# A gated recurrence and a feed-forward layer: a first state from 40 steps instead of 48, and the input products in five visits

## The chip, the core and the metric

The kernel runs on one core of a Trainium2 chip. The core has five engines with a queue each: TensorE (PE in the profile; its weight loads are shown apart as PEld), VectorE (DVE), ScalarE (ACT), GpSimd (POOL) and SyncE (SP). Each takes its instructions in the order in which they were written, and waits on semaphores where an instruction needs what another engine or a transfer makes. SBUF holds the tiles in use. PE writes its products to PSUM, from which DVE and ACT move them out. The metric is the time of one execution on the device, in microseconds (us), as the median of repeated runs. The profile is that of one more execution.

## The reference

Two sequences of 4096 vectors x of 256 numbers go through a gated recurrence with 64 states, a residual, a layer norm, a feed-forward layer with binarized weights, a residual and a layer norm.

```python
u = x @ W_in + b_in
g = sigmoid(x @ W_gate + b_gate)
def step(h_prev, inputs):
    u_t, g_t, x_t = inputs
    h_t = tanh(h_prev @ A + u_t @ Bm)
    y_t = h_t @ C.T + u_t @ D.T
    y_t = g_t * y_t + (1.0 - g_t) * x_t
    return h_t, y_t
...
x = layernorm(x + (ys @ W_out + b_out + x))
h = gelu(x @ bw1.T + b1)          # bw = mean|w| of its row * sign(w)
x = layernorm(x + (h @ bw2.T + b2))
```

## The kernel before, in words

**Segments and chunks.** Each sequence is cut into 64 segments of 64 steps. All 128 segments (two sequences times 64) are stepped side by side, so that one step of the recurrence is one product of 128 x 128 (`steps`, line 157: the matrix `ab` holds A above Bm, the moving operand `st[:, j]` holds h above u) and one tanh on ACT (line 158). Four steps of all segments are a chunk: `SPC` = 4, `NC` = 16 chunks, each of 512 vectors. A segment does not know its first state. It is therefore first run over its last `WARM` = 48 steps from zero. The state that this leaves at the end of segment k is copied (`first_states`, line 161) as the first state of segment k + 1, and then all 64 steps are run. At the end `compare` (lines 163 to 173) counts the entries where the last state of a segment agrees with the first state that was used for the next one within 2^-20. If not all agree, a serial branch at the end of the kernel does the recurrence and all chunks anew. There are 48 + 64 = 112 steps. The warm steps begin at chunk `FIRST` = (64 - 48) / 4 = 4.

**u.** The steps of a chunk need its u, which `u_of_chunks` (line 124) makes from x in transposed form (`x_tiles`): products on PE with 64 output columns (line 131), half of them into the upper and half into the lower 64 partitions of a PSUM tile of tag "h", then one eviction for each chunk that adds the bias and writes into `st` (lines 142 to 144, DVE except for one on ACT). One call takes one or two chunks.

**The opening.** The order of all instructions is written out by hand. `emit` (its costs are in `COST`) adds up the cost of the PE work that goes by and puts one step of the recurrence behind it whenever the sum passes a pace. In the opening this gives one step behind each part of the gate products. `parts` takes such parts from `gates` (its product is line 313; three 128-wide blocks to a part, two halves of 512 columns by two contractions to a chunk). The chunks come in the order 4, 5, 6, 7, 0, 1, 2, 3, 8, 9, 10 and on. A u visit is followed by one step. Between them stand the transfers on SP's queue: `load_xT` (x of a chunk, 512 KB, eight buffers), `load_weights`, `load_w` with `prepare_w` (signs and mean magnitudes of w1 and w2 on DVE), `halve_weights`, and for the first chunks `load_u`, `load_h` (u and h of a chunk into the tile hu), `load_n` (x by rows, xn).

**The chunks.** A chunk then goes through `mix` (line 374, ps_y = h C + u D, and d on DVE), `mix_end` (the gate, lines 386 and 389), `project` (line 399, W_out), the layer norm (`stats1`, `shift`, `norm`), a transpose (`turn` by PE for the first and the last chunks, `blocks` by DVE and sixteen transfers for the others, line 455), `up` (line 486), `low`, `down` (line 528), `add`, `stats` and `store`. POOL adds the bias rows (line 359) and takes the powers of the layer norms (line 265). The main loop runs over the chunks; steps of the recurrence that are left stand in it by up to four a chunk, and stop when all 112 are done. x of a chunk is loaded there a second time (`load_x`, line 338), and a third time for gates that are made there (`load_gate_x`).

**PSUM.** p_s holds the step's product. p_m holds one tile of two banks (tag "m": ps_y, ps_t). p_1 holds three tiles of one bank (tag "h": ps_u, ps_g, ps_h). p_2 holds one tile of two banks (tag "o": ps_o, and ps_z at first).

Of the kernel before, what the change touches and what calls it, by code (L numbers as in the profile page):

```python
# [8 lines left out]
FP = mybir.dt.float32  # L9
FR = mybir.dt.float32r  # L10
I32 = mybir.dt.int32
AF = mybir.ActivationFunctionType
ALU = mybir.AluOpType
# [3 lines left out]
P = 128  # L17
B, T, DM, S, H = 2, 4096, 256, 64, 1024
KD = DM // P
KH = H // P  # L20
SEG = 64
L = T // SEG
WARM = 48
N = 512
W = B * SEG
SPC = N // W
NC = L // SPC
TB = N // P
# [4 lines left out]
EARLY = 500  # L33
TOP, LOW = slice(0, S), slice(S, P)
# [3 lines left out]
def gated_recurrence_then_binary_ffn(  # L38
# [61 lines left out]
    def load_xT(c, pieces=1):  # L100
        x_tiles[c] = xp.tile([P, KD, N], FP, tag="xt", name=f"xt{c}", bufs=XTB)
        for k in range(pieces):
            cut = slice(k * KD // pieces, (k + 1) * KD // pieces)
            nc.sync.dma_start(out=x_tiles[c][:, cut, :], in_=xT[c][:, cut, :])
# [16 lines left out]
    nc.vector.tensor_scalar(bg_c, bias_c[:, 1 : 1 + KD], 0.5, None, ALU.mult)  # L121


    def u_of_chunks(*chunks):

        n = N * len(chunks) // 2
        parts = [(chunks[0], 0), (chunks[1], 0) if len(chunks) == 2 else (chunks[0], 1)]
        ps = p_1.tile([P, N], FP, tag="h", name=f"ps_u{chunks[0]}")
        for k in range(KD):
            for (c, i), r in zip(parts, (LOW, TOP)):  # L130
                nc.tensor.matmul(  # L131
                    ps[r, :n],
                    w_in[k],
                    x_tiles[c][:, k, bass.ts(i, n)],
                    start=k == 0,
                    stop=k == KD - 1,
                    skip_group_check=True,
                )
        for (c, i), r in zip(parts, (LOW, TOP)):
            to = u_of[:, bass.ds(c * SPC + i * n // W, n // W)].rearrange("p j b k -> p (j b k)")  # L140
            if r is TOP and c == FIRST:
                nc.scalar.activation(to, ps[r, :n], AF.Identity, bias=bin_c[r, :])
            else:
                nc.vector.tensor_scalar(to, ps[r, :n], bin_c[r, :], None, ALU.add)
        have_u.update(chunks)
        yield


# [31 lines left out]
    def load_weights():  # L180
        nc.sync.dma_start(out=cd, in_=CD)
        nc.sync.dma_start(out=w_out, in_=W_out)
        nc.sync.dma_start(out=bo_r, in_=b_out.partition_broadcast(P))
        nc.sync.dma_start(out=b2_r, in_=b2.partition_broadcast(P))

    def halve_weights():
        nc.vector.tensor_scalar(w_out, w_out, 0.5, None, ALU.mult)
        nc.vector.tensor_scalar(bo_r, bo_r, 0.5, None, ALU.mult)
# [12 lines left out]
    def load_w(n):  # L201
        half = bass.ts(n % 2, KH // 2)
        if n < 2:
            t = wk.tile([P, H], FP, tag="h", name=f"w1t{n}")
            nc.sync.dma_start(out=t, in_=w1T[:, n, :])
            t2 = wk.tile([P, KH // 2, DM], FP, tag="xhi", name=f"w1n{n}")
            nc.sync.dma_start(out=t2, in_=w1[:, half, :])
            w_tiles[n] = t, t2
        else:
            t = wk.tile([P, KH // 2, DM], FP, tag="h", name=f"w2t{n}")  # L210
            nc.sync.dma_start(out=t, in_=w2T[:, half, :])
            w_tiles[n] = t, None

    def prepare_w(n):
        half = bass.ts(n % 2, KH // 2)
        t, t2 = w_tiles[n]
        if n < 2:
            nc.vector.tensor_reduce(al1[:, half], t2, AX.X, ALU.add, apply_absolute_value=True)
            nc.vector.tensor_scalar(al1[:, half], al1[:, half], 1.0 / DM, None, ALU.mult)
            signs(sg1[:, n, :], t, f"a{n}")  # L220
        else:
            nc.vector.tensor_reduce(
                al2[:, n % 2, :],
                t.rearrange("p j d -> p d j"),
                AX.X,
                ALU.add,
                apply_absolute_value=True,
            )
            if n == 3:
                nc.vector.tensor_add(al2[:, 0, :], al2[:, 0, :], al2[:, 1, :])  # L230
            signs(
                sg2[:, half, :].rearrange("p j d -> p (j d)"),
                t.rearrange("p j d -> p (j d)"),
                f"b{n}",
            )
# [64 lines left out]
    def gates(chunks, size, x_of=lambda c: x_tiles[c.c]):  # L300

        room = size[0]
        for c in chunks:
            xt_ = x_of(c)
            c.t = wk.tile([P, KD, N], FP, tag="tg", name=f"tg{c.nm}", bufs=TGB)
            for m in range(KD):
                ps = p_1.tile([P, N], FP, tag="h", name=f"ps_g{c.nm}_{m}")
                for k in range(KD):
                    i = 0
                    while i < TB:  # L310
                        n = min(room, TB - i)
                        cut = bass.ds(i * P, n * P)
                        nc.tensor.matmul(  # L313
                            ps[:, cut],
                            w_gate[:, k, bass.ts(m, P)],
                            xt_[:, k, cut],
                            start=k == 0 and i == 0,
                            stop=k == KD - 1,
                            skip_group_check=True,
                        )  # L320
                        i += n
                        room -= n
                        if k == KD - 1 and i == TB:
                            later(c.tanh, m, ps)
                        if room == 0:
                            yield
                            room = size[0]
# [336 lines left out]
    def emit(what, pieces, pace=5600):  # L664
        nonlocal since
        for _ in pieces:
            since += COST.get(what, 0)
            if since >= pace:
                since = min(since - pace, pace // 2)
                if ready():  # L670
                    next_steps()
# [5 lines left out]
    def do(i, what, *args, pace=5600):  # L677
        if not 0 <= i < len(ch):
            return
        if what == "load":  # L680
            need = WARM + (ch[i].c + 1) * SPC
            while done < need:
                next_steps()
            ch[i].load_u()
            ch[i].load_h()
        elif what in ("load_n", "load_x", "load_gate_x"):
            getattr(ch[i], what)()
        else:
            emit(what, getattr(ch[i], what)(*args), pace)

    size = [3]
    stream = gates([ch[i] for i in (4, 5, 6, 7, 0, 1, 2, 3, 8, 9, *range(10, NC))], size)

    def parts(n, pace):
        emit("part", (next(stream) for _ in range(n)), pace)

    ET = mybir.EngineType
    with tc.manual_schedule(engines={ET.PE, ET.Activation, ET.DVE, ET.Pool, ET.SP}):
# [1 line left out]
        for c in range(FIRST + 1, FIRST + 6):  # L700
            load_xT(c)
        idle_products(7)
        emit("u", u_of_chunks(FIRST), 1 << 30)
        since = 0
        pairs = [(5, 6), (7, 8), (9, 10), (11, 12), (13, 14), (), (1, 2)]
        loads = [[10, 11], [12, 13], [14, 15, 0], [1, 2], [3], [], []]
        for n, pair in enumerate(pairs):
            before = 2 if n == 0 else 1
            parts(before, EARLY)
            if pair:  # L710
                emit("", u_of_chunks(*pair))
                if pair == (13, 14):
                    emit("", u_of_chunks(15, 0))
                emit("u", [None], EARLY)
            for c in loads[n]:
                load_xT(c)
            if n == 0:
                load_weights()
            if n == 3:
                halve_weights()  # L720
            if n >= 5:
                load_xT(n + 3)
                ch[n - 4].load_n()
                if n == 5:
                    ch[0].load_u()
                else:
                    ch[0].load_n()
                    ch[1].load_u()
                    ch[2].load_u()
            for i in range(7 - before):  # L730
                if 1 <= n < 5 and i == 0:
                    load_w(n - 1)
                if 2 <= n < 6 and i == 3:
                    prepare_w(n - 2)
                parts(1 if (n, i) != (6, 5) else 0, EARLY)
        assert done >= WARM + SPC, done
        emit("u", u_of_chunks(3), EARLY)
        for i in range(4):
            ch[i].xt = x_tiles[i]
        ch[0].in_x = ch[1].in_x = True  # L740
        do(10, "load_gate_x")
        parts(1, 600)
        do(0, "mix", pace=850)
        do(0, "mix_end")
# [25 lines left out]
        do(0, "rest")  # L770
        next(mixed)
        parts(3, 1700)
        for i in (4, 5):
            do(i, "load_x")
        end = len(ch) - 1
        parts_met = compare()
        since = -1 << 40
# [161 lines left out]
```

## Time and profile before

| what | value |
|---|---|
| median of 3 runs | 436.59 us (435.91 to 437.37) |
| the profiled execution | 438.51 us |
| its span, first to last instruction | 436.6 us |
| mean granted clock of TensorE | 0.993 |
| u products (L131), 6 to 75 us | 66 instructions, 15.1 us busy |
| gate products (L313), 6 to 75 us | 154 instructions, 43.1 us busy |
| step products (L157), 6 to 75 us | 124 instructions, 25.1 us busy |
| step tanh (L158), whole span | 112, median 270 ns, last start at 329.1 us |
| transfers of x in 512 KB (L104, L338) | 35, median 4.5 us from issue to landing |

How to read it: an fp32 product appears as two instructions on PE, so 62 steps are 124. Busy times of PE overlap, because a product is followed by the next before its end; the chain of waits shows what each adds. "Idle before, releaser" gives the time an engine stood before an instruction, and what ended it. The forty slices of the page show where the transfers are: nearly all of the first 55 us.

```profile
DMA  8877814400152624262426242524233232311102
```

### The profile page before, as it was taken

Reading aid. Unit: us, or ns where it says so; the run is one execution under the profiler, and the core shown is the slowest. Engines: PE = TensorE matmul, PEld = TensorE weight load, DVE = VectorE, ACT = ScalarE, POOL = GpSimd, SP = SyncE. Lnnn points to the kernel's source line nnn. Section 1 sums busy time; section 2 is a strip of 40 time slices with the busy share of each in tenths; the row PEclk is TensorE's granted clock in tenths of the full one; section 3 lists DMA queues with packets and bytes.
Section 4 is the critical chain, followed back from the end, with each engine's and each line's share of the span. In section 5 each row is a group of like instructions: output and inputs, shape, how many; then the busy total and the mean of one; then the engine's idle time right before and its main releaser. Section 6 shows DMA issues by size and latency. Waiting matters only on the chain.

```text
span 436.6 us, 6829 instructions
## 1 busy us (share of the span) xinstructions
PE 426.7 (98%) x2406; PEld 346.5 (79%) x2406; DVE 332.9 (76%) x569; ACT 285.3 (65%) x480; POOL 159.7 (37%) x176
## 2 busy tenths in 40 slices
PE   8999999999999999999999999999999999999992
PEld 6666666788887979787979797988888888888982
DVE  0235846886889898888888797979797979789684
ACT  2344352485768676767677776777768585849881
POOL 1000050373064545353524443444443444315513
PEclk9999999999999999999999999999999999999997
DMA  8877814400152624262426242524233232311102
GB/s 291 271 266 286 293 24 147 156 2 0 36 158 63 197 68 150 68 183 80 138 74 191 79 141 71 182 82 115 99 106 110 61 110 60 110 37 50 48 2 101
DMA packets 31479, 51.34 MB, mean 118 GB/s; under 512 B 5328, under 2 KB 19664, under 8 KB 31440
## 3 DMA queue, kind: packets, MB, share of 16 engines
q1 hardware_dynamic: 30864, 50.48, 36.5%
q8 instruction: 21, 0.34, 0.3%
q10 hardware_dynamic: 576, 0.37, 0.3%
q14 instruction: 18, 0.15, 0.1%
HBM read 31.43 MB, written 8.39 MB: 91 GB/s over the span
## 4 chain that ended last, share of the span: by engine, by line
PE 87%; DVE 4%; SPq 2%; ACT 2%; DMA 2%; issue 1%; POOL 1%; POOLq 0%; DVEq 0%
PE ps_h L486 24%; PE ps_o L528 23%; PE ps_g L313 13%; PE ps_z L399 12%; PE ps_s L157 6%; PE ps_y L374 6%; PE ps_u L131 3%; SPq L455 2%; DMA w_gate<-in_W_gate 1%; ACT xn L278 1%; DVE hlo L512 1%; DVE xlo L467 1%; DVE bs_a L255 1%; PE ps_t L430 1%; DMA hu<-st 1%
## 5 line engine op out<-in xcount | busy, mean ns | idle before, releaser
L528 PE MATMUL ps_o<-sg,hhi 128*128 128x256 f32 x496 | 120.7, 284 | 0.1
L528 PE MATMUL ps_o<-sg,hlo 128*128 128x256 f32 x496 | 117.9, 279 | 0.1
L496 ACT ACTIVATE h<-ps_h,bias_c,al 128x512 f32<-128x512 f32 x128 | 95.2, 770 | 15.0 <-PE ps_h L486 11.5
L528 PEld LDWEIGHTS ps_o<-sg,hhi 128*128 128x128 f32 x496 | 93.5, 188 | 1.6 <-DVE o L544 0.5
L528 PEld LDWEIGHTS ps_o<-sg,hlo 128*128 128x128 f32 x496 | 93.4, 188 | 1.5 <-DVE hlo L512 0.3
L486 PE MATMUL ps_h<-xhi,sg 128*128 128x512 f32 x256 | 92.6, 443 | 0.0
L359 POOL TENSOR_TENSOR xn<-xn,bo_r 128x256 f32<-128x256 f32 x64 | 58.1, 941 | 89.7 <-DMA xn<-in_x 84.1
L512 DVE TENSOR_TENSOR hlo<-h,hhi 128x1024 fp32r<-128x1024 f32 (+1 forms) x65 | 78.6, 1227 | 4.8 <-ACT hhi L505 4.6
L486 PE MATMUL ps_h<-xlo,sg 128*128 128x512 f32 x256 | 79.8, 393 | 0.0
L505 ACT CAST hhi<-h 128x1024 fp32r<-128x1024 f32 (+1 forms) x65 | 67.4, 1039 | 2.0
L313 PE MATMUL ps_g<-xt,w_gate 128*128 128x384 f32 (+3 forms) x212 | 67.5, 432 | 0.3 <-DMA w_gate<-in_W_gate 0.3
L265 POOL TENSOR_TENSOR rs_b<-rs_b,neg_half 128x4 f32<-128x4 f32 (+1 forms) x17 | 28.1, 1655 | 107.0 <-DVE rs_b L264 102.0
L486 PEld LDWEIGHTS ps_h<-xhi,sg 128*128 128x128 f32 x256 | 46.6, 189 | 18.6 <-issue 11.2
L158 ACT ACTIVATE st<-ps_s 64x128 f32<-64x128 f32 x112 | 30.0, 267 | 47.0 <-PE ps_s L157 46.6
L486 PEld LDWEIGHTS ps_h<-xlo,sg 128*128 128x128 f32 x256 | 48.1, 188 | 10.8
L157 PEld LDWEIGHTS ps_s<-st,wab 128*128 128x128 f32 x224 | 38.2, 191 | 21.5 <-ACT st L158 10.4
L359 POOL TENSOR_TENSOR xn<-xn,b_r 128x256 f32<-128x256 f32 x64 | 53.3, 863 | 1.9 <-PE ps_t L430 1.9
L399 PE MATMUL ps_z<-w_out,tg 128*128 128x256 f32 x224 | 50.7, 379 | 0.0
L399 PEld LDWEIGHTS ps_z<-w_out,tg 128*128 128x128 f32 x224 | 41.4, 190 | 5.1
L157 PE MATMUL ps_s<-st,wab 128*128 128x128 f32 x224 | 44.5, 280 | 0.0
L265 POOL TENSOR_TENSOR rs_a<-rs_a,neg_half 128x4 f32<-128x4 f32 x16 | 17.1, 1070 | 68.3 <-DVE rs_a L264 68.3
L278 ACT ACTIVATE xn<-xn,nm_a,rs_a 128x256 f32<-128x256 f32 x60 | 31.2, 590 | 16.1 <-DVE nm_a L270 16.1
(79 smaller groups left out, 484.3 us busy)
## 6 DMA issues: line engine op xcount, KB each, us to landing
xt<-in_xT SPq DMA_DIRECT2D x35, 512.0 KB, 4.5
xn<-in_x SPq DMA_DIRECT2D x16, 512.0 KB, 3.3
out_y<-xn SPq DMA_DIRECT2D x15, 512.0 KB, 2.6
xlo<-xb SPq DMA_DIRECT2D x208, 32.0 KB, 1.9
hu<-st SPq DMA_DIRECT2D x32, 128.0 KB, 2.3
w1t<-in_w1T SPq DMA_DIRECT2D x2, 512.0 KB, 5.4
w1n<-in_w SPq DMA_DIRECT2D x2, 512.0 KB, 7.1
w2t<-in_w2T SPq DMA_DIRECT2D x2, 512.0 KB, 5.7
```

What stands on the lines that cost most here:

```text
L157: nc.tensor.matmul(p_h, ab, st[:, j].rearrange("p b k -> p (b k)"), start=True, stop=True)
L158: nc.scalar.activation(h_of[:, j + 1].rearrange("p b k -> p (b k)"), p_h[TOP, :], AF.Tanh)
L265: nc.gpsimd.tensor_tensor(rs, rs, neg_half[:, cut], ALU.pow)
L278: nc.scalar.activation(r, r, AF.Identity, bias=self.sh[:, i : i + 1], scale=rs)
L313: nc.tensor.matmul(ps[:, cut], w_gate[:, k, bass.ts(m, P)], xt_[:, k, cut], start=k == 0 and i == 0, stop=k == KD - 1, skip_group_check=True,)
L359: nc.gpsimd.tensor_tensor(r[:, i, :], r[:, i, :], row, ALU.add)
L399: nc.tensor.matmul(self.ps_z[:, i, :], self.y[:, k, bass.ts(i, P)], w_out[:, k, :], start=k == 0, stop=k == KD - 1,)
L486: nc.tensor.matmul(ps, sg1[:, k, bass.ts(j, P)], part[:, k, :], start=n == 0, stop=n == 2 * KD - 1,)
L496: nc.scalar.activation(to, ps.rearrange("p (a i c) -> p a i c", a=P // 32, c=32) if self.far else ps, AF.Gelu, bias=b1_c[:, j : j + 1], sc ...
L505: nc.scalar.copy(hi[:, part, :], h[:, part, :])
L512: nc.vector.tensor_sub(lo[:, i, :], h[:, i, :], hi[:, i, :].bitcast(FP))
L528: nc.tensor.matmul(ps[:, i, :], part[:, j % 2, bass.ts(tb, P)], sg2[:, j, :], start=j == 0 and part is self.h[j // 2][0] and first, stop=j ...
```

## The change

The warm run has 40 steps instead of 48, so `FIRST` becomes 6 and the whole recurrence 104 steps. `u_of_chunks` takes a list of visits, each of one or two chunks, and makes them in one go: one visit in a tile of p_1 as before; two in the two halves of a tile `two` of p_m; a third in half a tile of p_2. After the first chunk, u is made in four goes, before the parts 3, 10, 25 and 40: (7, 8); (9, 10) and (11, 12); (13, 14) and (15, 0); (1, 2), (3, 4) and (5). The opening is written as 48 parts with a table (`AROUND`) of the transfers and weight preparations that stand beside each. The gates come in the order 6, 7, 8, 9, 0 to 5, 10 and on. The x tiles of chunks 0 to 5 are kept for the mix, where before it was those of 0 to 3; the loads of x of 4 and 5 ahead of the main loop go, as do second loads of 8 and 9 for their gates. In the changed file the lines below 144 stand nine lower.

```diff
-WARM = 48
+WARM = 40
...
-    def u_of_chunks(*chunks):
-
-        n = N * len(chunks) // 2
-        parts = [(chunks[0], 0), (chunks[1], 0) if len(chunks) == 2 else (chunks[0], 1)]
-        ps = p_1.tile([P, N], FP, tag="h", name=f"ps_u{chunks[0]}")
...
+    def u_of_chunks(*visits):
+
+
+        if len(visits) == 1:
+            rooms = [p_1.tile([P, N], FP, tag="h", name=f"ps_u{visits[0][0]}")]
+        else:
+            two = p_m.tile([P, KD, N], FP, tag="m", name=f"ps_u{visits[0][0]}")
+            rooms = [two[:, i, :] for i in range(KD)]
+        if len(visits) > 2:
+            more = p_2.tile([P, TB, DM], FP, tag="o", name=f"ps_u{visits[2][0]}")
+            rooms.append(more[:, 0 : N // DM, :].rearrange("p i d -> p (i d)"))
+        for chunks, ps in zip(visits, rooms):
+            n = N * len(chunks) // 2
+            parts = [(chunks[0], 0), (chunks[1], 0) if len(chunks) == 2 else (chunks[0], 1)]
+            for k in range(KD):
+                for (c, i), r in zip(parts, (LOW, TOP)):
+                    nc.tensor.matmul(
...
             for (c, i), r in zip(parts, (LOW, TOP)):
+                to = u_of[:, bass.ds(c * SPC + i * n // W, n // W)].rearrange("p j b k -> p (j b k)")
+                if r is TOP and c == FIRST:
+                    nc.scalar.activation(to, ps[r, :n], AF.Identity, bias=bin_c[r, :])
+                else:
+                    nc.vector.tensor_scalar(to, ps[r, :n], bin_c[r, :], None, ALU.add)
+            have_u.update(chunks)
         yield
...
-    stream = gates([ch[i] for i in (4, 5, 6, 7, 0, 1, 2, 3, 8, 9, *range(10, NC))], size)
+    stream = gates([ch[i] for i in (6, 7, 8, 9, 0, 1, 2, 3, 4, 5, *range(10, NC))], size)
...
+    VISITS = {
+        3: [[(7, 8)]],
+        10: [[(9, 10), (11, 12)]],
+        25: [[(13, 14), (15, 0)]],
+        40: [[(1, 2), (3, 4), (5,)]],
+    }
+    AROUND = {
+        3: [(load_xT, 12), (load_xT, 13)],
+        6: [(load_xT, 14)],
+        8: [(load_w, 0)],
+        11: [(load_xT, 15), (load_xT, 0)],
+        13: [(load_weights,)],
+        15: [(load_w, 1)],
+        17: [(load_xT, 1)],
+        18: [(prepare_w, 0)],
+        20: [(load_xT, 2)],
+        22: [(load_w, 2)],
+        23: [(halve_weights,)],
+        26: [(load_xT, 3), (load_xT, 4)],
+        28: [(prepare_w, 1)],
+        30: [(load_w, 3), (load_xT, 5)],
+        34: [(prepare_w, 2)],
+        36: [(ch[0].load_u,), (ch[1].load_n,)],
+        40: [(ch[1].load_u,), (ch[2].load_u,)],
+        42: [(prepare_w, 3)],
+        43: [(ch[0].load_n,), (ch[2].load_n,), (ch[10].load_gate_x,)],
+    }
...
-        pairs = [(5, 6), (7, 8), (9, 10), (11, 12), (13, 14), (), (1, 2)]
-        loads = [[10, 11], [12, 13], [14, 15, 0], [1, 2], [3], [], []]
-        for n, pair in enumerate(pairs):
...
+        for p in range(48):
+            for visit in VISITS.get(p, ()):
+                emit("", u_of_chunks(*visit))
                 emit("u", [None], EARLY)
+            for what, *args in AROUND.get(p, ()):
+                what(*args)
+            parts(1, EARLY)
         assert done >= WARM + SPC, done
-        emit("u", u_of_chunks(3), EARLY)
-        for i in range(4):
+        for i in range(6):
             ch[i].xt = x_tiles[i]
         ch[0].in_x = ch[1].in_x = True
-        do(10, "load_gate_x")
...
-        for i in (4, 5):
-            do(i, "load_x")
```

More of the change, by code (lines that the diff above doesn't have):

```diff
@@ L121, in gated_recurrence_then_binary_ffn @@
     nc.vector.tensor_scalar(bg_c, bias_c[:, 1 : 1 + KD], 0.5, None, ALU.mult)
-    def u_of_chunks(*chunks):
-        n = N * len(chunks) // 2
-        parts = [(chunks[0], 0), (chunks[1], 0) if len(chunks) == 2 else (chunks[0], 1)]
-        ps = p_1.tile([P, N], FP, tag="h", name=f"ps_u{chunks[0]}")
-        for k in range(KD):
-            for (c, i), r in zip(parts, (LOW, TOP)):
[L131 to L145, printed above, removed]
+    def u_of_chunks(*visits):
[13 more added lines that the diff above has]
+                    nc.tensor.matmul(
+                        ps[r, :n],
+                        w_in[k],
+                        x_tiles[c][:, k, bass.ts(i, n)],
+                        start=k == 0,
+                        stop=k == KD - 1,
+                        skip_group_check=True,
+                    )
+            for (c, i), r in zip(parts, (LOW, TOP)):
+                to = u_of[:, bass.ds(c * SPC + i * n // W, n // W)].rearrange("p j b k -> p (j b k)")
[4 more added lines that the diff above has]
+            have_u.update(chunks)
@@ L702, in gated_recurrence_then_binary_ffn @@
         idle_products(7)
-        emit("u", u_of_chunks(FIRST), 1 << 30)
+        emit("u", u_of_chunks((FIRST,)), 1 << 30)
         since = 0
-        pairs = [(5, 6), (7, 8), (9, 10), (11, 12), (13, 14), (), (1, 2)]
-        loads = [[10, 11], [12, 13], [14, 15, 0], [1, 2], [3], [], []]
-        for n, pair in enumerate(pairs):
[L708 to L713, printed above, removed]
-                emit("u", [None], EARLY)
[L715 to L735, printed above, removed]
+        for p in range(48):
+            for visit in VISITS.get(p, ()):
+                emit("", u_of_chunks(*visit))
+                emit("u", [None], EARLY)
+            for what, *args in AROUND.get(p, ()):
+                what(*args)
+            parts(1, EARLY)
         assert done >= WARM + SPC, done
-        emit("u", u_of_chunks(3), EARLY)
-        for i in range(4):
+        for i in range(6):
             ch[i].xt = x_tiles[i]
         ch[0].in_x = ch[1].in_x = True
-        do(10, "load_gate_x")
         parts(1, 600)
```

## The prediction

> **What bounds the kernel now.** I read the page's busy shares first, then the chain of waits in order of time, then the timeline of single engines where the chain touches the change.
>
> ```profile
> PE 426.7 (98%) x2406; PEld 346.5 (79%) x2406; DVE 332.9 (76%) x569; ACT 285.3 (65%) x480; POOL 159.7 (37%) x176
> PE 87%; DVE 4%; SPq 2%; ACT 2%; DMA 2%; issue 1%; POOL 1%; POOLq 0%; DVEq 0%
> ```
>
> TensorE (PE) has work for 98% of the span and is 87% of the chain that ended last. The chain tells what each piece costs PE, because its pieces lie end to end:
>
> ```profile
> 34.68 1.87 PE ps_u L131 x8
> 36.55 0.42 PE ps_s L157 x2
> 36.97 0.66 PE ps_g L313 x4
> 37.62 0.22 PE ps_s L157 x2
> ...
> 43.07 3.58 PE ps_u L131 x16
> 46.66 0.42 PE ps_s L157 x2
> ```
>
> One part of the gate (L313) takes 0.66 us and one step of the recurrence (L157) 0.22 us: a slot of 0.87 us that repeats without a gap. A visit to u (L131, eight instructions for two chunks) takes 1.87, and the step behind it 0.42 instead of 0.22. The double visit at 43.07 takes 3.58: its second half costs only 1.71, so 0.16 of each visit is the price of beginning it. From 6 to 75 us PE waited for data 0.3 us in all (for w_gate). So PE bounds the whole stage, and a step or a visit removed is a step or a visit gained. What VectorE (DVE) did beside the double visit:
>
> ```profile
> 45.02 1.52 DVE L144 TENSOR_SCALAR st<-ps_u,bias_c 64x512 f32<-64x512 f32 x2 [2.75 <-PE ps_u L131]
> 46.73 1.51 DVE L144 TENSOR_SCALAR st<-ps_u,bias_c 64x512 f32<-64x512 f32 x2 [0.20 <-PE ps_u L131]
> ```
>
> The first half's products end at 43.07 + 1.87 = 44.94; DVE begins to move them out 0.08 later and takes 1.52 for the two chunks, until 46.54. In that time PE already computes the second half, which has a PSUM tile of its own.
>
> In the main loop the interval from one ps_y to the next is one chunk:
>
> ```profile
> 288.17 1.72 PE ps_y L374 x4
> ...
> 310.68 1.72 PE ps_y L374 x4
> ```
>
> ```profile
> 332.81 1.88 PE L374 MATMUL ps_y<-hu,cd 128*128 128x512 f32 x4
> 354.50 1.88 PE L374 MATMUL ps_y<-hu,cd 128*128 128x512 f32 x4
> ```
>
> With four steps in it a chunk takes 22.51 us, without any 21.69 (the last step is at 327): 0.205 per step.
>
> **The change, part by part.** All of it is read from the order in which the built kernel's instructions stand, with the waits of each.
>
> *Steps.* 112 become 104. Up to the first ps_y the order has 53 instead of 56; in the main loop 39 instead of 44. The three that go first are those that stood behind a visit, at 0.42: −1.26. The five of the main loop go at 0.205 (one whole chunk of four, and the last step of the chunk before): −1.03. Without steps, the chain leaves PE at 347 and runs through DVE, POOL, the 16 transfers of L455 and back, 21.70 from one L467 (348.48) to the next (370.18). That is as long as PE's own 21.69, so the gain stops there, and it is whole.
>
> *Visits.* Behind the first, seven visits of 4 × 1.87 + 3.58 + 1.87 + 1.01 = 13.94 become four: 1.87 + 3.58 + 3.58 + (3.58 + 0.85) = 13.46, where 0.85 is the single chunk's 1.01 without the 0.16: −0.48.
>
> *The rooms, where a wait is added.* A visit of four or five chunks now takes its first two rooms from one tile, `two`, of p_m. In the built order the first product of the second room carries a wait for VectorE in each of the three large visits, and the count it waits for is that of the second eviction of the first room. The double visit of before has no such wait. So PE stands still from the end of the first room until DVE has moved both chunks out: 0.08 + 1.52, and then it starts again. Queued behind that instruction on PE is everything: the room's other products, the step, the gates. What a start costs from idle is not in the trace for this shape. The nearest row is the step at 85.43, which waited for ScalarE: 0.06 from its release, then 0.49 instead of 0.22. So the restart lies between 0.06 and 0.33. I take 0.15, nearer to the visit's 0.16 beginning, since it is the same product. Per visit 1.75 (1.66 to 1.93), for three visits +5.25 (4.98 to 5.79). The third room (p_2) waits only for its x.
>
> The Trainium skill says ("PSUM — Partial Sum Buffer", "PSUM bank collisions raise a hardware error") that accesses by two engines need guarding per bank and quadrant of partitions, and that one bank holds 512 fp32 columns. The two rooms are two banks, and the trace agrees that a product and an eviction in different banks may overlap (44.94 to 46.54 above). By that rule no wait is needed and the whole change would be −2.8; by the built order the wait is there, and I go by the order.
>
> *Moved steps.* With 0.873 a slot the large visits begin at about 19.6, 38.5 and 57.3 us, and the first ps_y at 71.8 (before: 68.26). On SP's queue: the first nine loads of x are issued as before, by 6.5, and their landings of up to 9.5 us end by 16, before 19.6. x of 15 and 0 wait for the u products of chunks 10 and 11 (21.5 and 24.7); issues here land in 3.1 to 8.8, so by 33.5, and gate 0 needs its x at 35. The four weights of `load_weights` (cd to b2_r) now stand behind x of 0, at 25 to 27; they landed in 7.7 to 9.3, so w_out is there by 35. DVE's `halve_weights` waits for it, and the evictions of the second large visit stand behind that on DVE, at 40.3: 5 us of cover; once gone, each us late is a us of PE. Both w1 loads and the first w2 are on time in the same way. The last w2 waits for DVE's `prepare_w(1)`, about 49, and holds x of 5 on SP's queue until then; 49.5 + 8.8 is 58, and chunk 5's products come at 62.6. `prepare_w(3)` (4.6 us: 1.9 + 0.4 + 2 × 1.1) now stands behind the last evictions, 65.3 to 69.9, before d of chunk 0 at 73.8. All this at nothing.
>
> *The gates' new order and the x loads saved* (8, 9 a second time, then 4 and 5: four issues of 512 KB): as many parts as before, each chunk's x in place as above. PE waited for none of the four loads, so nothing. POOL's queue keeps its order.
>
> *xn of chunk 0* moves from 50 to behind the h half of hu0, which waits for step 44 (64 us): issued at about 66, landing in 3.3 to 7.6. POOL then adds bo_r to chunks 0 and 1, eight additions, which before ran at 55.25 to 61.7, long before DVE's mix. Now they meet chunk 0's mix on DVE:
>
> ```profile
> 71.57 1.23 DVE L386 SCALAR_TENSOR_TENSOR d<-tg,d 128x1024 f32<-128x1024 f32 x1
> 72.83 1.22 DVE L389 SCALAR_TENSOR_TENSOR xt<-xt,d 128x1024 f32<-128x1024 f32 x1
> ...
> 74.18 1.92 PE L399 MATMUL ps_z<-w_out,xt 128*128 128x256 f32 x8
> ```
>
> ```profile
> 355.58 3.87 POOL L359 TENSOR_TENSOR xn<-xn,bo_r 128x256 f32<-128x256 f32 x4 [2.71 <-DMA xn<-in_x]
> 358.76 1.77 DVE L386 SCALAR_TENSOR_TENSOR d<-tg,d 128x1024 f32<-128x1024 f32 x1
> ```
>
> Beside POOL's addition L386 took 1.77 instead of 1.22, and L389 ends only 0.13 before ps_z: 0 to 0.42 late. I take 0.2.
>
> **The sum.** −1.26 − 0.48 − 1.03 + 5.25 + 0.2 = +2.7 us. The profiled execution had 438.51 us, of which the span is 436.6; it would become 441.2 (span 439.3). The runs' median, 436.59, is 1.9 below that execution, and the difference is put on the median: 439.3.
>
> **Rivals.** *The wait is hidden or void* (the change does what it says): without the 5.25 and with the 0.2 it is −2.6, 434.0. For it speaks that the double visit of before ran through. Against it: the steps behind a visit wait for its products by their order on PE, nothing else is queued between the rooms, and DVE cannot begin before the first room's last product, on which its wait lies. It decides from a stand below 0.86 us per visit (2.57 / 3), little more than one eviction. 8%.
>
> *The clock falls after each stand.* The first gate part took 1.65 us for two instructions that later take 0.65, at 6.57 us. If after each stand the second room ran at that pace, its 1.71 would be 4.3, and three times 2.6 more is 447. Against it: the stand of 0.5 us near 383 is followed by products at full speed. None of 1.7 us is there. 4%. The Trainium skill ("TensorE: Matmul & The Clock Gate", "HAM oscillation — how this bites in real kernels") puts the drop at idle gaps over some 3.4 us. By that rule these stands cost no clock, and the sum stays at +2.7; no row here shows a gap of either length.
>
> *A late load on SP's or DVE's queue* (w_out, x of 0 or 5, xn) beyond the covers above: 1 to 3 us more, 440.5 to 442. 10%.
>
> *Forty steps do not settle.* `compare` (L163 on) sends the kernel into the serial branch if a segment's first state is off by more than 2^-20 = 9.5e-7: 64 × 64 steps at some 0.87 us, over 3000 us more. The recurrence replayed in float32 on these inputs is off by at most 3.6e-7 after 40 steps, 4.6e-7 after 48, 2.0e-6 after 32. 1%.
>
> **Numbers.** The forecast as summed, 77%. Its own bounds are 436.59 − 2.77 + 4.98 = 438.8 and −2.77 + 5.79 + 0.42 = 440.0. The range 437.9 to 441.2 adds unseen small covers on both sides and most of the late loads; outside stay the first rival, the clock, the serial branch and the worst late load. Measurement tells 0.3%, 1.3 us, from nothing. Slower by more: all but the first rival (92%), less 5% for stands a third shorter than summed: 87%. Within: those 5% and 1% of the first rival. Faster: its other 7%.
>
> **What would show it.** In the changed profile: three stretches of about 1.6 us in which PE waits for DVE's L153 (L144 before), inside visits at about 21.5, 40.4 and 59.2; the first ps_y at 71.8; three steps fewer before it; the last step one chunk earlier, and four chunks at 21.7 instead of three. PE idle under 2 us in all there, or a first ps_y before 68, makes the forecast wrong; one after 73.5 says late loads or the clock.

## The result and the profile after

The changed kernel takes 440.81 us (440.30 to 441.57, 6 runs) against 436.77 (435.91 to 437.37, 6 runs) beside it: 1.0093 times as long, with a 95% interval of 1.0079 to 1.0107, or 4.0 us more. The profiled execution took 440.74 us.

The page of the changed kernel, its span, busy shares and chain by engine:

```profile
span 438.9 us, 6776 instructions
PE 423.1 (96%) x2390; PEld 343.0 (78%) x2390; DVE 333.5 (76%) x569; ACT 283.2 (65%) x472; POOL 161.6 (37%) x176
PE 89%; DVE 3%; SPq 2%; DMA 2%; ACT 1%; POOL 1%; issue 0%; POOLq 0%; DVEq 0%; ACTq 0%
```

PE has 3.6 us less to do than before (423.1 instead of 426.7), and yet the span is longer. What PE gained in work it lost in standing still. The chain of waits of the changed kernel (start, length, what) shows where:

```profile
18.31 1.89 PE ps_u L140 x8
...
20.23 0.76 DVE st L153
...
21.00 0.75 DVE st L153
...
21.79 1.94 PE ps_u L140 x8
23.73 0.42 PE ps_s L166 x2
```

```profile
71.11 0.86 PE ps_y L383 x2
```

A visit of four chunks is now cut in two: PE makes eight products, DVE moves out both chunks one after the other, and only then does PE make the other eight. From 18.31 to 23.73 that is 5.42 us, where the double visit of before took 3.58. The same is found at 37.24 and at 56.53. The first ps_y, which begins the first chunk's mix, comes at 71.11 instead of 68.26. The view of waits from 6 to 90 us (engine, line waited for: us in total, times, longest) names what ended them:

```profile
PEld ps_u L140 <- DVE st L153: 7.5, 3, 2.5
PE ps_u L140 <- DVE st L153: 4.9, 3, 1.6
```

Three stands (stretches in which PE stands still) of 1.6 us each, one for each large visit; no such row stands in the view of before.

### The profile page after: what moved, and what is told of

It is laid out like the page before. It is cut to its first block, busy times and chain, and to the rows that moved or that the text cites. A ratio compares the mean times of both kernels' runs of the same rounds, so it can differ in the third digit from the quotient of the medians.

```text
span 438.9 us, 6776 instructions
## 1 busy us (share of the span) xinstructions
PE 423.1 (96%) x2390; PEld 343.0 (78%) x2390; DVE 333.5 (76%) x569; ACT 283.2 (65%) x472; POOL 161.6 (37%) x176
## 4 chain that ended last, share of the span: by engine, by line
PE 89%; DVE 3%; SPq 2%; DMA 2%; ACT 1%; POOL 1%; issue 0%; POOLq 0%; DVEq 0%; ACTq 0%
PE ps_h L495 25%; PE ps_o L537 24%; PE ps_g L322 13%; PE ps_z L408 12%; PE ps_y L383 6%; PE ps_s L166 6%; PE ps_u L140 3%; SPq L464 2%; DMA w_gate<-in_W_gate 1%; DVE st L153 1%; PE ps_t L439 1%; ACT xn L287 0%; DMA xlo<-xb 0%; PE ps_p L537 0%; POOL rs_a L274 0%
## 5 line engine op out<-in xcount | busy, mean ns | idle before, releaser
L521 DVE TENSOR_TENSOR hlo<-h,hhi 128x1024 fp32r<-128x1024 f32 (+1 forms) x65 | 80.0, 1249 | 4.7 <-ACT hhi L514 4.4
L322 PE MATMUL ps_g<-xt,w_gate 128*128 128x384 f32 (+3 forms) x212 | 66.1, 425 | 0.5 <-DMA w_gate<-in_W_gate 0.5
L167 ACT ACTIVATE st<-ps_s 64x128 f32<-64x128 f32 x104 | 28.0, 269 | 50.4 <-PE ps_s L166 50.0
L368 POOL TENSOR_TENSOR xn<-xn,b_r 128x256 f32<-128x256 f32 x64 | 55.3, 894 | 1.9 <-PE ps_t L439 1.9
L166 PEld LDWEIGHTS ps_s<-st,wab 128*128 128x128 f32 x208 | 34.8, 189 | 18.8 <-ACT st L167 10.5
L166 PE MATMUL ps_s<-st,wab 128*128 128x128 f32 x208 | 40.7, 277 | 0.1
L472 ACT CAST xhi<-xlo 128x1024 fp32r<-128x1024 f32 x13 | 13.6, 1049 | 41.8 <-DMA xlo<-xb 21.2
L322 PEld LDWEIGHTS ps_g<-xt,w_gate 128*128 128x128 f32 x212 | 33.2, 191 | 7.7 <-issue 5.3
```

Source lines behind the costliest of these rows:

```text
L166: nc.tensor.matmul(p_h, ab, st[:, j].rearrange("p b k -> p (b k)"), start=True, stop=True)
L167: nc.scalar.activation(h_of[:, j + 1].rearrange("p b k -> p (b k)"), p_h[TOP, :], AF.Tanh)
L322: nc.tensor.matmul(ps[:, cut], w_gate[:, k, bass.ts(m, P)], xt_[:, k, cut], start=k == 0 and i == 0, stop=k == KD - 1, skip_group_check=True,)
L368: nc.gpsimd.tensor_tensor(r[:, i, :], r[:, i, :], row, ALU.add)
L521: nc.vector.tensor_sub(lo[:, i, :], h[:, i, :], hi[:, i, :].bitcast(FP))
```

## The experiments

The theory (A) is the prediction's: the two rooms in the two halves of one PSUM tile make PE wait for DVE, and everything else in the change gains what its products cost. Its first rival (B) is that something else about the visits, or the end of the kernel, decides. Two groups of kernels were run, each beside the kernel before; times of different groups are compared by their ratios to it.

**The kernel before, profiled once more.** The first profiled execution of before lay 1.9 us above the median of its runs. This looks at why.

> The kernel before, unchanged, profiled once more. The execution profiled first was 438.51 us, 1.7 above the median of the runs (436.77), and its gate parts ran at less than half pace until 10 us (first part 1.65 us, later ones 0.65), while those of the changed kernel ran at full pace from 7.8 us on. Theory A (a start that differs from execution to execution): the second profile has a faster start, the second u visit begins near 16.4 us instead of 17.9, and the span is near 435.1. Theory B (the start is a property of the kernel before): again 1.65 us for the first part and a span near 436.6.

It took 436.83 us in this one run, span 435.0. The chain at the start, first in the execution profiled before the prediction:

```profile
6.57 1.65 PE ps_g L313 x2
8.22 0.43 PE ps_s L157 x2
8.65 1.28 PE ps_g L313 x4
9.93 0.43 PE ps_s L157 x2
10.36 1.87 PE ps_u L131 x8
```

and then in this one:

```profile
6.24 0.84 PE ps_g L313 x2
7.08 0.30 PE ps_s L157 x2
7.39 0.66 PE ps_g L313 x4
8.04 0.22 PE ps_s L157 x2
8.27 2.66 PE ps_u L131 x8
```

In the first, a gate part of four instructions took 1.28 and a step 0.43, twice the 0.66 and 0.22 of later; in the second they ran at full pace from 7.39, though its second visit to u then waited for x. That visit ends at 12.23 in the one and at 10.93 in the other. From there to the first ps_y both take 56.03 (68.26 − 12.23 and 66.96 − 10.93), so 1.3 of the 1.6 us between the two spans arose in the first 12 us, and 0.3 behind the first ps_y. The like execution for the changed kernel, whose first gate part took 0.91 and whose first full step took 0.22, is this second one.

**Rooms in tiles of their own.** The second room is taken from p_2, the third from p_1, so that no two rooms share a tile. Nothing else changes. This kernel is called "own tiles" below.

```diff
-            two = p_m.tile([P, KD, N], FP, tag="m", ...)
-            rooms = [two[:, i, :] for i in range(KD)]
+            one = p_m.tile([P, KD, N], FP, tag="m", ...)
+            two = p_2.tile([P, TB, DM], FP, tag="o", ...)
+            rooms = [one[:, 0, :], two[:, 0 : N // DM, :].rearrange("p i d -> p (i d)")]
...
-            more = p_2.tile([P, TB, DM], FP, tag="o", ...)
-            rooms.append(more[:, 0 : N // DM, :].rearrange("p i d -> p (i d)"))
+            rooms.append(p_1.tile([P, N], FP, tag="h", ...))
```

> The changed kernel with a PSUM tile of its own for each room of a large visit (one from p_m, one from p_2, one from p_1). Theory A (the rooms of one tile make PE wait for the evictions): the three stands go, 1.84 + 1.87 + 1.88 = 5.6 us less than the changed kernel, 435.2 us, about 1.5 us faster than before. Theory B (PE would stand there anyway, for x, for DVE or for its own pipeline): no change, 440.8. Theory C (part of the loss is elsewhere): between the two.

It took 435.03 us (434.53 to 436.09, 7 runs), 0.9968 of before (0.9957 to 0.9980). Set against the changed kernel's 1.0093, that is 1.25% or 5.5 us less. Its chain:

```profile
17.60 3.58 PE ps_u L140 x16
21.19 0.42 PE ps_s L166 x2
...
34.70 3.58 PE ps_u L140 x16
...
52.12 4.45 PE ps_u L140 x24
```

and its timeline (start, length, engine, line, operation; in brackets the idle time before it and its releaser):

```profile
17.53 3.65 PE L140 MATMUL ps_u<-xt,wab 128*64 128x512 f32 x16
...
19.52 1.53 DVE L153 TENSOR_SCALAR st<-ps_u,bias_c 64x512 f32<-64x512 f32 x2 [6.99 <-PE ps_u L140]
```

Sixteen products run through while DVE empties the first room from 19.52 to 21.05. From the end of the second visit to the first ps_y the changed kernel takes 59.45 (71.11 − 11.66), this one 53.88 (64.84 − 10.96): 5.57, the three stands and nothing else. The Trainium skill ("PSUM — Partial Sum Buffer", "PSUM bank collisions raise a hardware error") asks for a guard by bank and quadrant, and not by address. The rows agree for two banks in different tiles; whether a product may also run beside an eviction in the other bank of the same tile was not tried, because there the wait is part of the built order.

**The stand put into the kernel before.** Only the double visit at 43 us, chunks (13, 14) and (15, 0), gets its two rooms from one tile.

```diff
+    pair_tile = []
...
-        ps = p_1.tile([P, N], FP, tag="h", name=f"ps_u{chunks[0]}")
+        if chunks[0] == 13:
+            pair_tile.append(p_m.tile([P, KD, N], FP, tag="m", name="ps_u13"))
+        if chunks[0] in (13, 15):
+            ps = pair_tile[0][:, (chunks[0] - 13) // 2, :]
+        else:
+            ps = p_1.tile([P, N], FP, tag="h", name=f"ps_u{chunks[0]}")
```

> The kernel before with one thing changed: the two halves of its one double visit, chunks 13, 14 and 15, 0, share a tile of p_m instead of two tiles of p_1. Theory A: one stand as in the changed kernel, +1.85 us, 438.6, and the double visit takes 5.4 us instead of 3.58. Theory B: no change, 436.8.

It took 438.81 us (438.53 to 439.10, 5 runs), 1.0047 of before (1.0033 to 1.0060): 2.0 us more. Its chain:

```profile
42.01 1.92 PE ps_u L138 x8
43.95 0.76 DVE st L151
44.72 0.75 DVE st L151
45.52 1.94 PE ps_u L138 x8
```

5.45 us instead of 3.58: one shared tile costs 1.87 in the visit, and the 2.0 between the medians says that it reaches the end. The stand needs none of the other parts of the change.

**The last visit three parts earlier.** The kernel with its own tiles, and the visit to (1, 2), (3, 4), (5) before part 37 instead of 40, so that the copy of the first states lies in another place.

```diff
-        40: [[(1, 2), (3, 4), (5,)]],
+        37: [[(1, 2), (3, 4), (5,)]],
```

> As the changed kernel with a tile for each room, and the last large visit stands at part 37 instead of 40, so that the copy of the first states on ScalarE (0.30 us), which follows step 40, lies beside the products of u. In the profile of the changed kernel step 41 came 0.3 us late behind that copy. Theory A: 0.3 us less than with the visit at 40, 434.9. Theory B (the late step is made up later, or x of chunk 5 or of 4 comes late for the earlier visit): the same or slower, 435.2 to 437.

It took 434.99 us (434.67 to 435.31, 5 runs), 0.9959 of before (0.9945 to 0.9973); with own tiles alone it was 0.9968, and the intervals overlap: the runs can't tell 0.3 us. In the trace the opening did become shorter: from the first gate part to the first ps_y 58.34 (65.01 − 6.67) instead of 58.67 (64.84 − 6.17). In this one execution the end is longer again. In the last 90 us PE waits like this:

```profile
PE ps_o L537 <- DVE o L553: 0.6, 1, 0.6
PE ps_h L495 <- ACT h L505: 0.4, 1, 0.4
```

With own tiles alone the same view has one row:

```profile
PE ps_h L495 <- ACT h L505: 0.4, 1, 0.4
```

So the copy's place is worth 0.3 us in the opening; whether any of it arrives is not shown.

**Six small visits instead of three large ones.** Own tiles, but u in single visits as before (each of two chunks, the last with the single chunk behind it), so that three visits more are begun and three more steps stand behind a visit.

```diff
-        10: [[(9, 10), (11, 12)]],
-        25: [[(13, 14), (15, 0)]],
-        40: [[(1, 2), (3, 4), (5,)]],
+        8: [[(9, 10)]],
+        15: [[(11, 12)]],
+        22: [[(13, 14)]],
+        29: [[(15, 0)]],
+        36: [[(1, 2)]],
+        43: [[(3, 4), (5,)]],
```

> As e1 (a tile for each room), but u in eight visits again: (9,10), (11,12), (13,14), (15,0), (1,2) and then (3,4) with (5) stand apart, seven behind the first, each followed by a step. Theory A (PE pays for each visit's beginning and for the dearer step behind it): three visits more cost 3 x 0.16 and three steps move from the main loop into the opening, at 0.42 instead of 0.205 each: +1.1 us, 436.1. Theory B (merging visits is worth nothing, the gain of e1 over before is the steps alone): 435.0.

It took 436.42 us (435.03 to 439.05, 12 runs), 0.9998 of before (0.9981 to 1.0014): 0.30% above own tiles' 0.9968, some 1.3 us, though the runs scatter so widely that the interval begins at 0.9981, barely above the 0.9980 at which that of own tiles ends. The trace is sharper. From the end of the second visit to the first ps_y it takes 55.64 (66.64 − 11.00), own tiles 53.88: 1.76 more, where the prediction's prices for three visits (0.48) and three steps behind them (1.26) sum to 1.74. From the first ps_y on it is 0.6 shorter (433.9 − 66.64 = 367.26 against 432.7 − 64.84 = 367.86), and three steps fewer are left for there (3 × 0.205 = 0.62).

**x of chunks 4 and 5 loaded again.** Own tiles, and the two loads that the change saves put back.

```diff
+        for i in (4, 5):
+            do(i, "load_x")
```

> As e1, with the second loads of x of chunks 4 and 5 put back ahead of the main loop (two transfers of 512 KB on SP's queue). Theory A (they are hidden, as nothing waits for them): no change, 435.0. Theory B (they hold up SP's queue, behind them the u and h of chunk 3, or share the transfers' rate): slower by up to the two issues' 1.0 us, 436.

It took 435.43 us (435.15 to 435.50, 5 runs), 0.9965 of before (0.9953 to 0.9978), against 0.9968 without them. Keeping x of 4 and 5 is worth nothing that can be measured. The second loads of 8 and 9, which the change also saves, were not put back.

**Eight steps put back.** Own tiles; when all 104 steps are done, the last step is done up to eight times again, in the places in which the kernel before would have had steps.

```diff
+REPEATS = 8
...
+    again = [REPEATS]
     def step():
         if ready():
             next_steps()
+        elif done == len(plan) and again[0] > 0:
+            again[0] -= 1
+            steps(plan[-1])
```

> As e1, and the last step of the recurrence is repeated eight times, at the places in the main loop where steps would stand in the next two chunks (the same state is written again). Theory A (PE bounds the main loop to its end): 8 x 0.205 = +1.64 us, 436.7. Theory B (without steps another chain, L464's transfers with DVE, ScalarE and POOL around them, is as long as PE's work, and what the steps free is lost again before the end): clearly less, +0.3 to +0.9, 435.3 to 435.9, and in the trace PE's waits for VectorE's and ScalarE's work in the last 60 us grow smaller.

It took 436.13 us (435.87 to 438.20, 12 runs), 0.9991 of before (0.9979 to 1.0003): 0.23% or 1.0 us above own tiles, with intervals that just touch. That lies between the whole price of eight steps (8 × 0.205 = 1.64) and the nothing of a hidden edit; the traces tell where the rest went. PE's timeline with the steps put back (its lines stand one lower),

```profile
352.49 1.88 PE L384 MATMUL ps_y<-hu,cd 128*128 128x512 f32 x4
374.19 1.88 PE L384 MATMUL ps_y<-hu,cd 128*128 128x512 f32 x4
```

and with own tiles alone:

```profile
350.20 1.88 PE L383 MATMUL ps_y<-hu,cd 128*128 128x512 f32 x4
371.89 1.88 PE L383 MATMUL ps_y<-hu,cd 128*128 128x512 f32 x4
```

From the first ps_y to the last of these it takes 308.76 (374.19 − 65.43) against 307.05 (371.89 − 64.84): the eight steps cost 1.71 there, 0.21 each, in full. From there to the end it is the other way round: 60.11 (434.3 − 374.19) against 60.81 (432.7 − 371.89). The kernel that came earlier gives 0.70 back in its last 60 us. With the steps put back, the view of waits has no row for PE's products in the last 90 us; the row of 0.4 that own tiles has there is gone.

## Why the prediction held, and where its sum was short

The measured 440.81 lies within the range, 1.5 us above the 439.3. The mechanism was the one named: three stands that wait for DVE's L153, and three steps fewer before the first ps_y. They came 0.7 to 1.3 us earlier than forecast (first ps_y at 71.11 for 71.8), because this execution began faster than the one that was read. But the sum was short: a gain of 0.8 us was booked that isn't there, a small wait was missed, and the restart after a stand was put too low. The sum's own bounds, 438.8 to 440.0, don't hold the 440.81. The range does, because it was widened for late loads and small covers; of these a small one came, and that the lost gain found room there too is luck.

**The base.** The sum of +2.7 was made against the profiled execution (436.6 to 439.3 us of span) and the difference then put on the median. The changed kernel's span, 438.9, seems to meet the sum, but by an accident: the execution profiled first had the slow start shown above, and the changed kernel's had not. Against the second profile of before, the difference is 438.9 − 435.0 = 3.9 us, as between the medians. So it was right to put the difference on the median, and the sum itself was 1.2 us short.

**The three stands** were forecast at 1.75 each, 5.25 in all (4.98 to 5.79). They took 5.42 − 3.58 = 1.84, 5.45 − 3.58 = 1.87 and 6.31 − 4.43 = 1.88: 5.59. In the first one the evictions took the 1.52 of the forecast, and DVE began 0.03 after the products instead of 0.08. The restart was mis-sized: 0.04 passed from DVE's end, and behind it the eight products took 1.94 instead of 1.71, so it cost 0.27 where 0.15 was taken. The last 0.02 is the first room's, 1.89 instead of 1.87.

**Visits and steps in the opening**, −0.48 and −1.26, were right: 1.74 against the 1.76 that their return cost.

**The opening as a whole.** The second visit now stands a gate part and a step later than before (0.88), so that the 56.03 of before compares, like for like, with 55.15. The changed kernel's 59.45 is 4.30 more: −1.74, +5.59, and 0.44 for two steps that are late.

**The missed wait** is most of this 0.44. ACT's copy of the first states stands behind step 40. Before, it fell beside a u visit. Now it falls between two gate parts, as the timeline of the changed kernel shows:

```profile
53.63 0.27 ACT L167 ACTIVATE st<-ps_s 64x128 f32<-64x128 f32 x1 [0.60 <-PE ps_s L166]
53.93 0.30 ACT L170 COPY st<-st 64x126 f32<-64x126 f32 x1
54.33 0.46 PE L166 MATMUL ps_s<-st,wab 128*128 128x128 f32 x2
```

The next step waits for the copy: 0.08 of idle time and 0.46 instead of 0.22, so 0.32; with the visit at part 37, where the copy lies beside products of u, it is gone. The other 0.12 is a step at 12.72 that took 0.34. It is the fifth, the first that needs u of chunk 7, and DVE moves out 7 and 8 from 11.71 to 13.24; that it waited for the first half of this is likely, but no run tried it. The prediction counted every step that goes and none that comes to stand elsewhere with its cover gone.

**POOL's additions beside the mix** were taken at 0.2 and cost nothing. The timeline of the changed kernel:

```profile
68.95 5.57 POOL L368 TENSOR_TENSOR xn<-xn,bo_r 128x256 f32<-128x256 f32 x8 [67.16 <-DMA xn<-in_x]
73.09 1.22 DVE L390 TENSOR_TENSOR d<-ps_y,xt 128x1024 f32<-128x1024 f32 x1 [3.95 <-PE ps_y L383]
74.42 1.23 DVE L395 SCALAR_TENSOR_TENSOR d<-tg,d 128x1024 f32<-128x1024 f32 x1
```

POOL is done at 74.52, when L395 has only begun. The lower bound of the term was the right one.

**The five steps of the main loop** were booked at −1.03, with the words that the gain "is whole". This is the term that failed. From the first ps_y to the last listed one the changed kernel is 0.79 shorter than before (378.17 − 71.11 = 307.06 against 374.81 − 66.96 = 307.85; why not 1.03 wasn't found), and of that 0.54 is lost in what follows (438.9 − 378.17 = 60.73 against 435.0 − 374.81 = 60.19). What arrives is 0.25. That is no more than single executions differ by: from the first ps_y to the end, the kernel before took 368.34 in one (436.6 − 68.26) and 368.04 in the other (435.0 − 66.96), the changed kernel 367.79 (438.9 − 71.11). So the sum below takes 0.25, and the runs say only that well under 1.03 arrives. The loss at the end is firmer. Behind the last listed ps_y, the four profiled executions with the steps of before or with eight put back took 60.11 to 60.40, the five with fewer steps 60.73 to 61.25. In the last 90 us of the changed kernel PE waits:

```profile
PE ps_o L537 <- DVE o L553: 0.4, 1, 0.4
PE ps_h L495 <- ACT h L505: 0.3, 1, 0.3
```

In the second profile of before the one such row there is 0.2. The prediction had seen that the other chain, through DVE, POOL and the sixteen transfers and back, takes 21.70 for a chunk beside PE's 21.69, and inferred that the gain stops there whole. But two chains of equal length leave no room for a gain on one of them: what PE comes earlier, it may stand for later. The steps put back fit this reading. It isn't the whole account: with six small visits PE reaches its last listed ps_y 306.32 (372.96 − 66.64) after the first, another 0.73 sooner than with own tiles, and yet its end, 60.94, is hardly longer than own tiles' 60.81. Which link of that chain holds PE at the very end was not told apart.

The sum then reads −1.26 − 0.48 + 5.59 + 0.44 for the opening, −0.25 behind it, and a start 0.15 earlier (4.15 between the first ps_y of the two like executions against 4.30): +3.9. Against the forecast's +2.7 that is 0.78 of lost gain, 0.44 of late steps and 0.34 of stands more, less 0.2 for POOL and 0.15 for the start: 1.2.

**The rivals.** The wait was neither hidden nor void; without it the kernel takes 0.9968 of before, as own tiles show, less of a gain than the rival's 434.0, for which the late steps (0.44) and the end (0.78) account. The clock didn't fall after a stand; windows before, in and behind the first one (busy times of PE, PEld, DVE, ACT and POOL, the granted clock, DMA share, GB/s):

```profile
18.00:20.00 2.00, 2.00 (x11) 0.60 (x9) 0.00 (x0) 0.27 (x1) 0.00 (x0) 1.00 0.79 297
20.30:21.70 1.40, 0.00 (x0) 0.00 (x0) 1.39 (x2) 0.00 (x0) 0.00 (x0) 1.00 0.35 76
21.80:23.70 1.90, 1.90 (x9) 0.52 (x9) 0.00 (x0) 0.00 (x0) 0.00 (x0) 1.00 0.53 203
```

More telling than the clock's column are the durations: the products behind the stand took 1.94, not the 4.3 of that rival, and the step behind them 0.42 as after any visit. No load came late, since the opening's 4.30 is used up by the terms above, and the only transfer for which PE waits there from 6 to 90 us is w_gate's, 0.5 at the start; and forty steps were enough, for 440.8 us have no room for the serial branch.

## What to carry to other kernels

When two pieces of work are put into one tile to save a start, ask which of the tile's readers the next writer will wait for: here three starts at 0.16 and three steps behind a visit at 0.42 were saved, and each large visit paid 1.84 to 1.88 for it, until the rooms got tiles of their own. When a step is taken out or moved, look for what else now stands without cover. And where a second chain takes as long as the busiest engine, a gain on that engine need not be whole: price it by the time to the very end of the kernel, not by the interval in which it arises.

## What the runs showed of the hardware

One and the same kernel begins differently in two executions: the first gate part took 1.65 us in one and 0.84 in the other, and the next part 1.28 against 0.66, at a granted clock that the windows give as 1.00 in both. The Trainium skill ("TensorE: Matmul & The Clock Gate", "The HAM clock gate (the "warmup" mystery)") says that the first products run at half the clock for a time that varies from run to run, because the window that watches them doesn't begin with the kernel. The doubled durations agree with that, the windows' clock column doesn't show it.

A stand of 1.6 us on PE cost 0.23 to 0.24 us beyond itself in the products that followed, in three visits of one kernel and, at 1.94 behind 1.92, in the one visit of another.
